# Edge counting of a graph layer: border groups copied by GpSimd, last counts and decode rearranged, hints at a branch

## The chip, the cores and the metric

The program runs on one core of one Trainium2 chip. A core has five engines that run their own instruction streams and meet at semaphores: TensorE (PE in the profile; its weight loads are PEld), VectorE (DVE), ScalarE (ACT), GpSimd (POOL) and SyncE (SP, which here issues most DMAs). The metric is the time of one execution on the device in microseconds. A run's time is the span of the profiled instructions and a little around it.

## The reference, cut to what matters

The network is a two-layer graph attention network on 625 nodes with 20000 edges, followed by a transformer block with a mixture of experts. The change lies in the first part of the first graph layer:

```python
ei = _add_self_loops(edge_index, n)             # 20000 edges, sorted by dst, and 625 loops
src, dst = (ei[0], ei[1])
xl = (x @ W).reshape(n, heads, out_ch)          # x is layer-normalized; 625x768 @ 768x1024
alpha_src = jnp.einsum('nhc,hc->nh', xl, a_src)
alpha_dst = jnp.einsum('nhc,hc->nh', xl, a_dst)
e = jax.nn.leaky_relu(alpha_src[src] + alpha_dst[dst], 0.2)
m = jax.ops.segment_max(e, dst, num_segments=n)
e = jnp.exp(e - m[dst])
s = jax.ops.segment_sum(e, dst, num_segments=n)
msg = xl[src] * (e / (s[dst] + 1e-16))[:, :, None]
out = jax.ops.segment_sum(msg, dst, num_segments=n)
```

The same layer also needs the residual product `h0 @ Wr1 + br1`, of the same size as `x @ W`.

## The kernel before

The kernel has no list of edges in its attention. It first builds a dense matrix `C` of 625 x 625 counts (how often source s points at target d), held as five tiles of 125 targets, and then does attention as dense work with `C` as a weight: a score is masked where `C` is 0 and its exponential is multiplied by `C`.

**Counting.** The edges are laid out as 160 columns of 125 edges, in `G` = 40 groups of `GJ` = 4 columns, sorted by target. For one column, `count` (line 258) makes two small matrices and multiplies them on PE into the accumulator `cps`, five PSUM banks, one for each tile of targets: `target` (line 254, always DVE) makes `oh`, a 125 x 125 one-hot row of the target with a weight, and `step` (line 246) makes a 125 x 210 step function of the source, on ACT or on DVE. The sum over edges of steps, differenced along the columns, is a histogram. To need 210 columns instead of 625, three thirds of the sources share a column with the weights 1, 256 and 65536 (`places`, line 263, gives weight and place), and `decode` (line 492) takes the three fields apart again with rounding on DVE and ACT.

A group goes to the tile in which its first target lies; its index is read into a register of PE (`some`, line 434). A group that reaches over the border between two tiles must be counted for the next tile too. `overlaps` (line 328) finds for each of the four borders the last group that begins below it: it makes a one-hot row `selg` over the groups, GpSimd multiplies it into the three arrays `past`, `upper` and `dst` (twelve products), and DVE reduces these to `rest`. The 16 columns of `rest` are the last counts.

**What runs between the counts.** The first 90 us of the span interleave the counts with the layer norm (`deviation`, `normalized`), the transposes of the normalized rows (`turn_y`), the product with W1 (`project1`: for each of 5 tiles two halves of 512 columns, 12 products in the trace for each half), the sums with the attention vectors (`dots`, DVE) and their transposes (`spread`). PE, DVE and ACT are under a manual schedule here: their instructions stand in the order in which the code calls them, so an instruction that waits holds up all behind it on its engine. `oh` and `step` tiles come from rings of `AHEAD` = 24 buffers. All PSUM results of this stage that aren't counts use three buffers, `pps`.

After the last counts the code runs `residual1(0)`, the decode of the five tiles, `residual1(1)` and the first scores of tile 0 (`lifted`, ACT and then DVE). Each `residual1` is one half of the residual product of tile 0, 12 products in the trace; what it returns is ACT's copy of the result to `pr`, called later.

**The branch.** `examine` tests that the edges are sorted and that no pair occurs so often that a field overflows. If not, the `If` at line 536 counts again in a safe way, 2684 instructions over the engines that this input never runs; every engine reads `oki` and jumps over its own part. Behind it stand `Messages` of tile 0 (`neg` at line 589, the masked maximum at 596, exp at 599, the weighing at 602), `project_residual(1)` on PE (`ph`, line 173) and the transposes of the weighed scores (`tpz`, line 616).

## Time and profile before

| | us |
|---|---|
| median of 3 runs | 1011.8 (1011.01 to 1015.82) |
| the profiled execution | 1011.31 |
| its span | 1009.0 |
| PE busy in the span | 958.5 |
| DVE, ACT, POOL busy | 457.9, 297.3, 68.4 |
| counting stage up to the last count | 0 to 90.9 |
| decode (first copy of `cps` to last field) | 93.7 to 104.6 |
| first transposes of weighed scores, `tpz` | 120.9 |

In the lists in order of time a row gives the start and the duration in us, the engine, the line, the operation with what it writes and reads, its shape, and in brackets how long the engine had been idle and what ended that. Instructions of one form that follow each other are one row (x12), whose duration runs from the first start to the last end. The duration of one DVE or ACT instruction is longer than its distance to the next, since neighbours overlap by some tenths of a microsecond. Fields that end in q (PEq) are an engine's instruction sequencer.

### The profile page before, as it was taken

What the parts mean: (1) busy time and instruction counts of PE and PEld (TensorE: products, weight loads), DVE (VectorE), ACT (ScalarE), POOL (GpSimd) and SP (SyncE); (2) the same over time, 40 slices, a digit from 0 to 9 for tenths busy, and PEclk for the clock granted to TensorE, in tenths of its full rate; (3) what the DMA queues carried; (4) which work ended last, traced back from release to release, by engine and by line L of the source; (5) the groups of instructions that cost most, each with busy time, mean ns of one, the idle gap of its engine ahead of it and who ended that gap; (6) DMA issues with size and microseconds to landing.
All of it is one profiled execution on the core that took longest, in us unless ns stands there. A gap on an engine that the chain in (4) does not pass through costs nothing. (4 is left out here: it accounts for less than half of the span.)

```text
span 1009.0 us, 15158 instructions
## 1 busy us (share of the span) xinstructions
PE 958.5 (95%) x4655; PEld 588.9 (58%) x4656; DVE 457.9 (45%) x1331; ACT 297.3 (29%) x777; POOL 68.4 (7%) x140
## 2 busy tenths in 40 slices
PE   7999799999999999999999889999999999989995
PEld 4565464777655556677775555545455655544553
DVE  8888775584194840485555454121210122221303
ACT  4897552552131120444442211002110212011302
POOL 1000000000000010000000022110100110200001
PEclk9999899999999999999999789999999999999998
DMA  9404100301410174999300579500489999999994
GB/s 276 161 1 168 34 1 24 117 1 46 87 24 1 55 182 83 404 406 379 136 2 1 222 221 358 168 18 25 162 316 317 353 366 408 341 403 365 406 404 156
DMA packets 87726, 191.69 MB, mean 190 GB/s; under 512 B 34404, under 2 KB 36316, under 8 KB 87673
## 3 DMA queue, kind: packets, MB, share of 16 engines
q1 hardware_dynamic: 80441, 175.22, 49.0%
q0 software_dynamic: 7152, 15.64, 5.3%
q8 instruction: 29, 0.48, 0.2%
q10 hardware_dynamic: 80, 0.16, 0.1%
q14 instruction: 24, 0.20, 0.1%
HBM read 213.29 MB, written 39.55 MB: 251 GB/s over the span
## 5 line engine op out<-in xcount | busy, mean ns | idle before, releaser
L1309 PE MATMUL pw<-ew,hT 128*64 128x384 f32 (+1 forms) x672 | 160.1, 487 | 6.3 <-PEq L1629 2.1
L1309 PEld LDWEIGHTS pw<-ew,hT 128*64 128x64 f32 (+1 forms) x672 | 101.3, 160 | 59.5 <-issue 15.3
L1283 PE MATMUL ph<-ew,xid 128*64 128x512 f32 (+1 forms) x432 | 127.7, 594 | 3.4 <-DMA ew<-in_L_ffn_W_dram 1.8
L1299 ACT ACTIVATE hT<-tph,bT 128x64 f32<-128x64 f32 (+1 forms) x168 | 41.0, 361 | 289.0 <-PE tph L1294 194.2
L1283 PEld LDWEIGHTS ph<-ew,xid 128*64 128x64 f32 (+1 forms) x432 | 53.6, 155 | 66.8 <-issue 59.7
L1286 DVE COPY hb<-ph 128x512 f32<-128x512 f32 x30 | 20.6, 688 | 139.1 <-PE ph L1283 139.1
L629 PE MATMUL agg<-xl,zT 125*125 125x256 f32 (+1 forms) x300 | 79.8, 417 | 1.5 <-ACT zT L618 1.4
L629 PEld LDWEIGHTS agg<-xl,zT 125*125 125x125 f32 x300 | 54.5, 188 | 19.8 <-ACT zT L618 2.8
L398 PE MATMUL pp<-w,yT 128*125 128x512 f32 x120 | 55.0, 609 | 0.1
L1346 DVE TENSOR_TENSOR rw<-rw,pw 64x192 f32<-64x192 f32 (+1 forms) x48 | 12.9, 315 | 91.0 <-PE pw L1309 90.7
L734 PE MATMUL ph<-wr,h1T 128*125 128x384 f32 x160 | 52.8, 486 | 0.0
L693 PE MATMUL ph<-w,h1T 128*125 128x384 f32 x160 | 52.4, 486 | 0.0
L249 ACT ACTIVATE step<-halved,past 125x210 f16<-125x210 f16 x138 | 50.9, 459 | 0.0
L173 PE MATMUL ph<-wr,yT 128*125 128x512 f32 x96 | 44.9, 625 | 5.2 <-PEq L536 2.8
L958 DVE CUSTOM_DVE_ANT_0 e<-sc,later 125x625 f32<-125x625 f32 (+4 forms) x60 | 29.9, 543 | 36.2 <-PE sc L942 36.2
L1025 PE MATMUL po<-wpj,aT 128*125 128x384 f32 x120 | 42.8, 505 | 0.4 <-DVE xx L1029 0.4
L962 ACT ACTIVATE e<-e,of 125x625 f32<-125x625 f32 (+4 forms) x60 | 35.7, 596 | 23.3 <-DVE of L958 23.3
L693 PEld LDWEIGHTS ph<-w,h1T 128*125 128x125 f32 x160 | 30.0, 188 | 21.1 <-issue 0.5
L734 PEld LDWEIGHTS ph<-wr,h1T 128*125 128x125 f32 x160 | 29.8, 188 | 20.8
L876 PE MATMUL pv<-L_ffn_Wv,hT 128*125 128x384 f32 x120 | 39.5, 486 | 0.0
L913 PE MATMUL pq<-hT,L_ffn_Wq 128*128 128x313 f32 (+1 forms) x144 | 39.4, 429 | 0.0
L913 PE MATMUL pq<-hT,L_ffn_Wk 128*128 128x313 f32 (+1 forms) x144 | 39.4, 429 | 0.0
(350 smaller groups left out, 1278.1 us busy)
## 6 DMA issues: line engine op xcount, KB each, us to landing
ew<-in_L_ffn_W_dram SPq DMA_DIRECT2D x108, 1536.0 KB
xr<-zt SPq DMA_DIRECT2D x5, 3076.0 KB
xg<-zt SPq DMA_DIRECT2D x5, 3072.0 KB
w<-in_L_gnn_W_dram SPq DMA_DIRECT2D x4, 1536.0 KB
wr<-in_L_gnn_Wr_dram SPq DMA_DIRECT2D x4, 1536.0 KB
xid<-xg POOLq DMA_DIRECT2D x40, 96.0 KB, 9.4
b2b<-in_L_ffn_b_dram SPq DMA_DIRECT2D x9, 384.0 KB
rw<-xr POOLq DMA_DIRECT2D x14, 192.2 KB
```

What stands on the lines that cost most here:

```text
L173: nc.tensor.matmul(pp[:R, :], yT[:, c, cols(t)], part(wr1, KD, c, i, 512), start=(c == 0), stop=(c == KD - 1))
L249: nc.scalar.activation(o, halved[:, :n], AF.Sign, bias=at, scale=-1.0)
L398: nc.tensor.matmul(pp[:R, :], yT[:, c, cols(t)], part(w1, KD, c, i, 512), start=(c == 0), stop=(c == KD - 1))
L629: nc.tensor.matmul(self.agg[:R, c0:c0 + n], zT[:, s, :], xl[:, s, x0:x0 + n], start=(s == 0), stop=(s == T - 1))
L693: nc.tensor.matmul(ph[:R, :384], h1T[:, c, cols(t)], part(w2, KH, c, i, 384), start=(c == 0), stop=(c == KH - 1))
L734: nc.tensor.matmul(ph[:R, :384], h1T[:, k, cols(t)], part(wr2, KH, k, i, 384), start=(k == 0), stop=(k == KH - 1))
L876: nc.tensor.matmul(pp[:R, :384], hT[:, c, cols(t)], w[i][:, c, :], start=(c == 0), stop=(c == KD - 1))
L913: nc.tensor.matmul(pp[:, :b - a], w[:, c, c0:c0 + 128], hT[:, c, a:b], start=(c == 0), stop=(c == KD - 1))
L1025: nc.tensor.matmul(po[t, i][:R, :384], aT[:, c, cols(t)], wpj[i][:, c, :], start=(c == 0), stop=(c == KD - 1))
L1283: mm = nc.tensor.matmul(ph[g * M:(g + 1) * M, :C].rearrange("p (j f) -> p j f", f=128), self.xT[:, k, :], w[:, k, g], start=(k == 0), stop ...
L1299: self.made = nc.scalar.activation(hT[c][:, k, r], tp[:, k, r], AF.Relu, bias=self.bT[:, f:f + 1])
L1309: mm = nc.tensor.matmul(pw[i][g * M:(g + 1) * M, :384], hT[c][:, k, g * M:(g + 1) * M], w[:, self.block(c, g, k), i * 384:(i + 1) * 384], ...
```

## The change

- **Border groups.** The arrays `upper`, `past` and `edges` get one more group in front, set to 0 by GpSimd. `overlaps` counts on DVE, with one comparison and one reduce, the groups that begin below each border; GpSimd reads each count into a register and copies that group's four columns out of the three arrays. The reduces and products of before are gone.
- **Last counts.** In tile 4 both copies of `xl` come right after the products. Then follow `residual1(0)`, `dots(4)`, the last three groups, the copy to `pr`, `spread(4)`, the 16 counts of `rest`, and then `residual1(1)`, whose copy to `pr` is called after the decode. The first scores `zs` are made before the decode. `expert_biases` (two transposes, a copy to `bT_all`) stays right before the decode and so stands behind `residual1(1)`.
- **Decode.** ACT copies 210 columns of a tile to SBUF (`s`), and DVE subtracts there. Three tiles are copied before the first subtraction; their steps are then interleaved across tiles.
- **Branch hints.** Two prefetch hints for the `If` are put in the streams of DVE and ACT, beside the last tile's first field. PE's stream gets none.
- **Zero products.** Twenty products of zeros (`WARM`) are added into `cps` after the self loops' counts.
- **Order at the start.** `tl`, `tli` and `drel` come before the layer norm of tile 0, and `places` is split: two operations before the normalized rows, three after.
- `examine` sums within its comparison.

```diff
@@ zero products, arrays with a group of zeros in front
+            for i in range(WARM):
+                nc.tensor.matmul(cps[:, i % T, :SH + 1], zeros[:, :R], zeros[:, :SH + 1], start=False,
+                                 stop=False, skip_group_check=True)
-            edges = etile([2 * G, GJ], "edges")
...
+            edges = etile([2 * G + 1, GJ], "edges")
...
+            padded = {n: etile([G + 1, GJ], n) for n in ("upper", "past")}
+            upper, past = (padded[n][:, 1:, :] for n in ("upper", "past"))
+            for a in (*padded.values(), edges):
+                nc.gpsimd.memset(a[:, :1, :], 0.0)
+            dev = deviation(0)
+            placing = places(src, upper, past)
+            next(placing)
+            y = normalized(0, *dev)
+            for _ in placing:
+                pass
@@ overlaps
-                for t in range(1, T):
-                    below = op_.tile([R, G], F32, name="below", bufs=2)
-                    nc.vector.tensor_scalar(below, tl, float(t), None, op0=OP.is_lt)
-                    nc.vector.tensor_reduce(cnt[:, t - 1:t], below, AX.X, OP.add)
...
-                nc.vector.tensor_tensor(selg, iog, cnt[:, :, None].to_broadcast([R, T - 1, G]),
-                                        op=OP.is_equal)
...
-                        nc.gpsimd.tensor_mul(m, a.rearrange("p g j -> p j g"),
-                                             selg[:, t, None, :].to_broadcast([R, GJ, G]))
-                        parts.append((rest[i][:, t, :], m))
...
+                below = etile([T - 1, G], "below")
+                nc.vector.tensor_tensor(below, tl[:, None, :].to_broadcast([R, T - 1, G]),
+                                        tile_no[:, :, None].to_broadcast([R, T - 1, G]), op=OP.is_lt)
...
+                nc.vector.tensor_reduce(cnt, below, AX.X, OP.add)
+                cnti = op_.tile([1, T - 1], I32, name="cnti", bufs=1)
+                nc.vector.tensor_copy(cnti, cnt[0:1, :])
...
                 for t in range(1, T):
+                    last = nc.values_load(cnti[0:1, t - 1:t], engines=[mybir.EngineType.Pool],
+                                          min_val=0, max_val=G)
+                    for r, a in zip(rest, (padded["past"], padded["upper"], edges)):
+                        nc.gpsimd.tensor_copy(r[:, t - 1, :],
+                                              a[:, ds(last, 1), :].rearrange("p o j -> p (o j)"))
+                    nc.gpsimd.tensor_scalar_add(rest[2][:, t - 1, :], rest[2][:, t - 1, :],
                                                 -float(t * R))
@@ the end of the counting stage
-            for _ in check:
-                pass
-            expert_biases()
-            nc.scalar.activation(small.tile([R, 1], F32, name="sd"), eps[:R], AF.Exp)
-            dots(T - 1)
             copied = residual1(0)
+            dots(T - 1)
+            some(3)
+            copied()
+            spread(T - 1)
+            for t in range(1, T):
+                for j in range(GJ):
+                    count(cps[:, t, :SH + 1], *(r[:, t - 1, j:j + 1] for r in rest), j < GJ - 1)
+            nc.scalar.activation(small.tile([R, 1], F32, name="sd"), eps[:R], AF.Exp)
+            copied = residual1(1)
+            zs = [lifted(rows, al, 0, h) for h in range(HEADS)]
+            for _ in check:
+                pass
+            expert_biases()
@@ decode
-                nc.scalar.copy(d, cps[:, t, 1:SH + 1])
-                nc.vector.tensor_tensor(d, cps[:, t, :SH], d, op=OP.subtract)
+                s = ah.tile([R, SH + 1], F32, name="s", bufs=T)
+                nc.scalar.copy(s, cps[:, t, :SH + 1])
+                yield
+                nc.vector.tensor_tensor(d, s[:, :SH], s[:, 1:], op=OP.subtract)
...
+                    if t == T - 1 and k == 2:
+                        for ins in (lowered.ins, made.ins):
+                            with tc.issue_after(ins):
+                                tc.mark_branch_hint_location("general", hint="LikelyTaken",
+                                                             engines=[ins.engine])
@@ the five tiles
-            copied()
-            spread(T - 1)
-            copied = residual1(1)
-            zs = [lifted(rows, al, 0, h) for h in range(HEADS)]
+            going = [decode(t) for t in range(T)]
+            for d in going[:3]:
+                next(d)
+            for t in range(T + 2):
+                for i in range(min(t, T - 1), -1, -1):
+                    next(going[i], None)
+                if t + 3 < T:
+                    next(going[t + 3])
             copied()
             ok = nc.values_load(oki[0:1, 0:1], min_val=0, max_val=1)
-            with tc.If(ok == 0):
+            with tc.If(ok == 0, label="general"):
```

## The prediction

> **What bounds the kernel now.** I read the page first, then the list of waits of TensorE (PE), then the order of time of the first 165 us, then windows of 1 us and of 3.41 us around the one slow place.
>
> ```profile
> span 1009.0 us, 15158 instructions
> PE 958.5 (95%) x4655; PEld 588.9 (58%) x4656; DVE 457.9 (45%) x1331; ACT 297.3 (29%) x777; POOL 68.4 (7%) x140
> ```
>
> PE is busy 95% of the span. The instructions behind the `If` stand in the same order on every engine in both programs, so only the first 121 us can change, and whatever PE gains there moves the rest with it.
>
> ```profile
> PE tpy L390 <- DVE y L309: 3.8, 1, 3.8
> PE ph L173 <- PEq L536: 2.8, 1, 2.8
> PE ph L173 <- ACT pr L407: 2.3, 1, 2.3
> ```
>
> These are PE's three longest waits (total, times, longest): for the first normalized tile, for the branch of the `If`, for ACT's copy of half a residual. The order of time (start, us, engine, line) shows what surrounds them:
>
> ```profile
> 10.70 1.51 PE L390 MATMUL tpy<-ident,y 125*128 125x125 f32 x6 [3.83 <-DVE y L309]
> 12.15 6.87 PE L398 MATMUL pp<-w,yT 128*125 128x512 f32 x12
> 25.83 0.80 PE L390 MATMUL tpy<-ident,y 125*128 125x125 f32 x6
> ...
> 80.07 5.33 PE L398 MATMUL pp<-w,yT 128*125 128x512 f32 x12
> 85.24 5.74 PE L260 MATMUL cps<-step,oh 125*125 125x210 f16 x36
> ...
> 97.05 5.32 PE L173 MATMUL ppr<-wr,yT 128*125 128x512 f32 x12
> 104.71 1.12 PE L173 MATMUL ph<-wr,yT 128*125 128x512 f32 x2 [2.35 <-ACT pr L407]
> 108.64 12.39 PE L173 MATMUL ph<-wr,yT 128*125 128x512 f32 x22 [2.81 <-PEq L536]
> ```
>
> Twelve 512-wide products take 5.33 us, but 6.87 at 12.15; 22 of them at 108.64 take 12.39 where 22/12 x 5.33 is 9.8. The windows of 1 us (PE, PEld, DVE, ACT, POOL, then the granted clock) say why the second is slow:
>
> ```profile
> 106.00:107.00 1.00, 0.00 (x0) 0.00 (x0) 0.98 (x2) 1.00 (x2) 0.00 (x0) 1.00 0.09 25
> 108.00:109.00 1.00, 0.36 (x1) 0.39 (x2) 0.99 (x2) 0.57 (x2) 0.00 (x0) 0.50 0.03 8
> 113.00:114.00 1.00, 1.00 (x3) 0.44 (x2) 0.96 (x5) 0.68 (x1) 0.33 (x1) 0.50 0.40 129
> 115.00:116.00 1.00, 1.00 (x4) 0.42 (x3) 0.96 (x4) 0.11 (x2) 0.00 (x0) 1.00 0.88 344
> ```
>
> After a thin stretch of PE the clock is 0.50 for some 6.8 us.
>
> **The change, part by part** (times on the clock of the profile before).
>
> *Zero products and the earlier y.* DVE now does `tl` (0.15 + 0.67), `tli` (0.17) and `drel` (0.30) in its 1.6 us wait for x, and only two of `places` (0.15 apart) while ACT makes `sd` (9.13 to 9.42). The reciprocal starts at 9.47 instead of 9.77, so y ends at 10.34, 0.3 earlier. PE is idle from 6.86 to 10.70 now. Twenty zero products at the spacing of the five at L243 ((1.14 - 0.39)/4 = 0.19 us) fill 3.8 of these 3.84 us. PE is then busy from 4.08 on. Before, it was busy from 10.70 on and its products went from 0.85 to 0.43 us apart at about 15.0, so 4.3 us of work suffice. I take full speed from y on: the transposes cost 0.80 instead of 1.51. With y at 10.34 the first copy of `yT` starts near 10.9 and the products near 11.4 instead of 12.15, and the twelve cost 5.33 instead of 6.87: 0.75 + 1.54 = **2.3 us**. If the zeros end late, at 10.7, 0.3 is lost; if the clock doesn't rise, all but 0.3. The weights cover this: by the windows 2.94 MB had arrived by 12.0, and dst, src, x and half of W1 are 2.2 MB; the other half makes 3.75 MB, which had arrived by 14.0 and is wanted at 17.7. The tile still ends on ACT (11 steps, 4.07 us, then the copies of `yT`).
>
> *Border groups on GpSimd.* Gone from DVE: eight `below`/`cntg` (0.16 us apart on average, 1.3), `selg` (0.33), twelve reduces (0.22 apart, 2.7), four adds (0.36), two reduces of `examine` (0.67 each). New: three DVE operations (about 0.8) and, on GpSimd, three small memsets, four register loads, twelve copies of 125x4, four adds. No row shows a GpSimd operation addressed by a register: 0.16 us (the iota of 125x5) below, 0.62 (the largest product there now) above; I take 0.6, nearest to two-input work of this engine, 12 us for 20 steps. They start at 15.3 and are wanted at 93.8, and behind them in GpSimd's queue wait only `be1` and `br1`, wanted after 112. So 0 on the path. The DVE time saved is worth 0 too: tiles 1 to 3 run at 14.3 us each (44.73, 59.06, 73.74) with PE full. Below nothing it can't go while PE hides it; the first tile's wait is ACT's.
>
> *Last counts and decode.* From 80.07, using the rows above: project1 ends at 85.40, eight counts (0.09 apart) and the transposes of `al` end at 86.5, `residual1(0)` runs to 91.75. Meanwhile ACT copies `xl` (0.59), DVE makes `dots(4)` (eight at 0.35, to 88.9), then twelve `oh` and a step (to 92.0); ACT's eleven steps (0.37 apart) end at 91.2. PE's twelve counts and `spread(4)` end at 93.3. Now a new wait: ACT's copy of `rows` stands before its twelve border steps, so these run from 93.85 to 98.3, and PE gets its 16 counts at that pace, to 98.5 (they ended at 90.8). Queued behind them on PE is `residual1(1)` (5.2, to 103.65) and the transposes for `bT_all` (0.25). ACT's `Exp` load (1.28) and four z (0.735 apart) fit in until 102.7. ACT then waits for `bT_all`, so the first copy of `cps` starts at 104.2 instead of 93.69. The decode took 10.9 us (93.69 to 104.60) with gaps on DVE; with three tiles copied ahead it's paced by DVE's five operations, 1.46 us a tile (`d` and `r` 0.60, the other three 0.87, by their starts from 101.55 to 103.01): 0.3 + 5 x 1.46 + 0.5 = 8.1, to 112.3 with ACT's copy of `pr` at its end. The subtraction from SBUF instead of PSUM shows no row; the like one with all in SBUF (L506, 0.37) stands beside 0.38, so 0.
>
> PE takes its branch at 103.9: 2.8 us as now, no hint stands on its queue. The first half of `project_residual(1)` runs 106.7 to 111.8; the second waits for that copy of `pr` (the instruction order gives it this wait) and runs 112.35 to 117.5. DVE meets its branch at 112.2. Its stall now is 2.77 us (109.0 to 111.76, L589); with the hint I take 0.5 (bounds 0 and 2.8, since no row shows a hinted branch here). z of head 0 is complete 3.2 us after `neg` starts (111.76 to 114.99), so at 115.9, before 117.5. Transposes of z thus start at 117.5 instead of 120.87: **3.4 us**. DVE then lags PE by some 3.4 us more than before; it idles 1.1, 1.5, 1.3 and 1.8 us at 122, 141, 143 and 148, and no part of its work comes later than in the profile before, so I count nothing there.
>
> *Sum*: 2.3 + 3.4 = 5.7. The profiled execution took 1011.31 (span 1009.0 and 2.3 around it), so 1005.6; the median of the runs is 0.5 above it, so **1006.1**.
>
> *The clock* is the open term. PE in the 16 counts does 1.4 us of work in 5.2, with no pause over 0.6. Windows of 3.41 us on the grid of the drop (114.05) give both ends: 103.81 to 107.22 with 1.12 us busy lost the clock, 837.67 to 841.08 with 1.56 busy (46%) kept it, but 557.78 to 561.19, with tiny products, lost it at 2.10. Bounds 0 and 3.4 us (a drop of 6.8). I take 0, as the counts never stop for long, and give the other end a large chance.
>
> The Trainium skill ("TensorE: Matmul & The Clock Gate", Part 1 on the clock gate) says that the clock falls after an idle window of about 3.4 us. By this rule the counts keep the clock and the sum is 5.7. Here the window at 103.81 was a third busy and lost it all the same, so the rule alone doesn't settle it.
>
> **The rivals.**
>
> *The clock falls in the counts.* Then `residual1(1)` runs at half speed for 3.4 to 5.2 us of its time and the decode starts 1.7 to 3.4 late; or it falls at PE's branch, 2.8 idle, and the half of `project_residual(1)` behind it loses 1.7, of which 0.5 is covered. Gain 2.3 to 4.0: 1007.8 to 1009.5. For it speaks the window at 103.81; against it, 837.67.
>
> *The hints do nothing.* DVE stays 2.8 at its branch, z of head 0 comes at 118.2, of head 1 at 119.9; PE waits 0.7 and then some 1.7: gain 3.3, 1008.5. For it: the stalls on PE and DVE are alike (2.81, 2.77) and both begin when the engine has finished its own work, so more than a fetch may be in them.
>
> *GpSimd is late* (slower). If a step with a register costs c, the borders are ready at 15.3 + 20c and wanted at 93.8: it decides from c = 3.9 us on, six times the 0.62 of the row. It is slower by 0.5% from c = 4.5 on; at 5 us it is 21.5 late, 1027.6. Only the lack of any such row speaks for it.
>
> **How the numbers follow.** A measurement of this kernel can tell about 0.5% (5 us) from no change. Forecast 0.55 (own range 1003, where the border steps hold PE up less, to 1007.5, where the zero products bring 0.9; most of it below 1006.7), clock 0.28, no help of the hints 0.10, GpSimd 0.07. Faster: 0.50 from the forecast and 0.03 from the edges of the others, 0.53; same: 0.05 + 0.27 + 0.08 = 0.40; slower 0.07. The range leaves out GpSimd and a little at each end: 1002.0 if the border steps didn't pace PE at all (PE's own work ends 4 us earlier), 1010.7 halfway between the clock's far end alone (1009.5) and with the hints' 2.4 on top (1011.9).
>
> **What would show it.** Right: `tpy` at 10.4 with 0.8 us and its products 5.3; 16 counts spread over 5 us beside ACT's steps; the first copy of `cps` near 102 and `neg` near 110.5 on the new clock, idle before it under 1 us; transposes of z near 115.2; clock 1.00 throughout. Wrong: a 0.50 window between 90 and 116; PE waiting for `rest`; DVE still 2.8 idle at L544; the second half of `project_residual(1)` not waiting for `pr`, which would make it faster than I say.

## The result, and the profile after

The changed kernel takes 1014.7 us (median of 20 runs, 1012.29 to 1018.23), beside 1011.8 for the kernel before (20 runs): a ratio of 1.0029, 95% interval 1.0017 to 1.0040. The forecast was 1006.1 with a range from 1002.0 to 1010.7, so the change is 2.9 us slower where 5.7 faster was forecast. The profiled execution took 1013.89 us, 2.6 more than that of before: 1.3 in the span (1010.3) and 1.3 outside it (3.6, before 2.3).

The page, and from the list of PE's waits the two longest and the one for ACT's steps:

```profile
span 1010.3 us, 15200 instructions
PE 962.9 (95%) x4675; PEld 592.1 (59%) x4676; DVE 451.7 (45%) x1309; ACT 297.3 (29%) x777; POOL 64.3 (6%) x147
```

```profile
PE ph L174 <- ACT pr L410: 3.2, 1, 3.2
PE agg L637 <- ACT zT L626: 2.7, 5, 1.5
...
PE cps L261 <- ACT step L250: 1.6, 2, 1.0
```

The waits for `y` (now 0.4) and for the branch are gone from the top; a wait for `zT`, 0.3 at this place before, has grown to 1.5. PE in order of time (start, us, engine, line):

```profile
10.43 0.86 PE L393 MATMUL tpy<-ident,y 125*128 125x125 f32 x6 [0.39 <-DVE y L316]
11.53 5.42 PE L401 MATMUL pp<-w,yT 128*125 128x512 f32 x12 [0.24 <-ACT yT L387]
...
92.10 4.47 PE L261 MATMUL cps<-step,oh 125*125 125x210 f16 x16 [1.03 <-ACT step L250]
96.36 6.22 PE L174 MATMUL ppr<-wr,yT 128*125 128x512 f32 x12
102.42 0.33 PE L433 MATMUL tb<-ident,bb 96*128 96x96 f32 x2
102.89 5.38 PE L174 MATMUL ph<-wr,yT 128*125 128x512 f32 x12
111.51 7.11 PE L174 MATMUL ph<-wr,yT 128*125 128x512 f32 x12 [3.23 <-ACT pr L410]
118.46 0.71 PE L624 MATMUL tpz<-ident,z 125*125 125x125 f32 x5
119.64 0.81 PE L624 MATMUL tpz<-ident,z 125*125 125x125 f32 x5 [0.48 <-DVE z L610]
121.98 4.11 PE L637 MATMUL agg<-xl,zT 125*125 125x256 f32 x10 [1.53 <-ACT zT L626]
...
133.49 1.88 PE L174 MATMUL ph<-wr,yT 128*125 128x512 f32 x4
```

The start is 2.1 us earlier (`tpy` of tile 1 is at 23.76, before at 25.83), where 2.3 was forecast. The transposes `tpz` start at 118.46, 2.4 earlier than before. By the next residual product all of it is lost: it begins at 133.49, where the kernel before had it at 132.23. From the first `tpz` to the first `agg` it is 3.5 us; before it was 1.5:

```profile
120.87 1.25 PE L616 MATMUL tpz<-ident,z 125*125 125x125 f32 x10
122.41 2.42 PE L629 MATMUL agg<-xl,zT 125*125 125x256 f32 x10 [0.29 <-ACT zT L618]
```

Three rows of twelve or ten products are too long, 6.22, 7.11 and 4.11 us, where the same products take 5.32, 5.38 and 2.32 at full clock. Windows of 1 us (PE, PEld, DVE, ACT, POOL, granted clock, then DMA) show why:

```profile
95.00:96.00 1.00, 0.98 (x4) 0.70 (x4) 0.00 (x0) 1.00 (x3) 0.00 (x0) 0.50 0.00 0
112.00:113.00 1.00, 1.00 (x2) 0.33 (x1) 0.00 (x0) 0.00 (x0) 0.00 (x0) 0.50 0.04 16
123.00:124.00 1.00, 1.00 (x4) 0.81 (x3) 1.00 (x2) 0.93 (x2) 0.00 (x0) 0.50 0.00 0
```

Between 90 and 130 us the clock falls three times, for 3.4 us each, and each time behind a thin stretch of PE; before it fell there once, for 6.8 us. And ACT in order of time shows what `agg` waits for:

```profile
118.90 0.82 ACT L607 ACTIVATE z<-z,m 125x625 f32<-125x625 f32 x1 [0.89 <-DVE m L606]
120.54 0.82 ACT L607 ACTIVATE z<-z,m 125x625 f32<-125x625 f32 x1 [0.82 <-DVE m L606]
121.27 0.66 ACT L626 COPY zT<-tpz 125x625 f32<-125x625 f32 x1
```

The transposes of head 0 are done at 119.17, but their copy stands in ACT's queue behind the fourth exponential, and that waits for DVE's fourth maximum. DVE is late for two reasons: its last work ahead of the branch ends at 111.40 (before at 108.99), and its stall at the branch did not shrink:

```profile
114.72 0.49 DVE L597 TENSOR_SCALAR neg<-C 125x625 f32<-125x625 f32 x1 [3.32 <-DVEq L544]
```

### The profile page after: what moved, and what is told of

The parts are those of the page before. It is cut to its first block, busy times and chain, and to the rows that moved or that the text cites. A ratio compares the mean times of both kernels' runs of the same rounds, so it can differ in the third digit from the quotient of the medians.

```text
span 1010.3 us, 15200 instructions
## 1 busy us (share of the span) xinstructions
PE 962.9 (95%) x4675; PEld 592.1 (59%) x4676; DVE 451.7 (45%) x1309; ACT 297.3 (29%) x777; POOL 64.3 (6%) x147
## 5 line engine op out<-in xcount | busy, mean ns | idle before, releaser
L742 PEld LDWEIGHTS ph<-wr,h1T 128*125 128x125 f32 x160 | 29.8, 188 | 20.8
```

What stands on the lines that cost most here:

```text
L742: nc.tensor.matmul(ph[:R, :384], h1T[:, k, cols(t)], part(wr2, KH, k, i, 384), start=(k == 0), stop=(k == KH - 1))
```

## The experiments

All ran in five rounds beside the kernel before. As the time outside the span turned out to differ between kernels, each result has the median span and the median of what lies outside it. The kernel before has spans of 1008.8 to 1010.5 in these comparisons with 1.9 outside; the changed kernel has 1012.0 and 3.3. Since the span of one and the same kernel moves by 1.7 us between comparisons, a difference of a microsecond between kernels of different comparisons is not shown; where it matters, the span is given against the before of the same comparison. For the changed kernel that is about 2.1 longer (an estimate: the before's 1011.8 less its 1.9 outside is 1009.9).

### The parts alone

**Order at the start and zero products, put alone into the kernel before:**

```
+WARM = 20                       # 20 zero products behind the self loops' counts
-            dev = deviation(0)  # before tl
...
+            dev = deviation(0)  # behind drel; places() split around normalized(0)
```

> The kernel before with only the start of the change: twenty zero products, the tile numbers ahead of the layer norm, places in two parts. In the first runs the time outside the profiled span was 1.9 us for the kernel before and 3.3 to 3.6 for all kernels with the zero products, 1.6 without them. My theory: the zero products take 2.2 us out of the span (1010.5 to 1008.3) and put 1.5 us on the time outside it, so the time is 1011.2 to 1012 against 1012.4 before. Rival: the time outside the span belongs to something else in the change; then it stays at 1.9 and the time is near 1010.2.

Measured: 1011.5 us, ratio 0.9997 (0.9986 to 1.0008); span 1007.4, 1.4 shorter than the before's in this comparison, but 3.7 outside. In its profiled execution the first products of tile 4 start at 73.73, as before (73.74), since the clock falls on the way:

```profile
28.59 7.11 PE L407 MATMUL pp<-w,yT 128*125 128x512 f32 x12
```

The part gains in the span less than its 2.2 us, and all that it gains is lost again outside.

**The changed kernel without its zero products** (`WARM = 0`):

> The changed kernel without the twenty zero products. My theory: the zero products work as predicted, so without them the transposes of the first normalized rows take 1.5 us and the first twelve products 6.9, and the time rises by 1.5 to 2.5 us to 1016.2 to 1017.2. Rival: what starts earlier is lost again at the decode (the clock falls at another place); then the time changes by less than 0.7 us.

Measured: 1016.1 us, ratio 1.0042 (1.0029 to 1.0056); span 1014.35, 1.6 outside. Against the before of its comparison the span is 3.85 longer, and 3.45 in `zero_in_if` below, the other kernel that doesn't run the products; with them it is some 2.1. So the zero products are worth 1.4 to 1.8 us of the span (`start_only` has 1.4), and 1.7 comes back outside. The six spans here lie between 1010.6 and 1016.2, so these sizes are rough.

**The border groups, put alone into the kernel before** (the new `overlaps`, padded arrays, `tile_no`):

> The kernel before with only the border groups copied by GpSimd. My theory: nothing of it is on the path in the first 80 us; at the last counts VectorE has 1.5 us less to do ahead of its last one-hots (five reduces and the adds), so they end 0.5 to 1.5 us earlier, and the time is 0 to 1.5 us less than before. Rival (GpSimd late with its register loads and copies): TensorE waits for rest and the time rises by more than 2 us.

Measured: 1011.0 us, ratio 1.0004 (0.9995 to 1.0013); span 1009.2, 1.6 outside. The 36 last counts run from 85.09 in 5.74 us, as before. Worth nothing, as forecast. In the changed kernel's trace GpSimd's 16 operations, with the register loads between them, lie between 16.34 and 20.78 us, some 0.22 us a step where I took 0.6.

### The branch

**Without the hints:**

```
-                    if t == T - 1 and k == 2:
-                        for ins in (lowered.ins, made.ins):
-                            with tc.issue_after(ins):
-                                tc.mark_branch_hint_location("general", hint="LikelyTaken", ...)
```

> The changed kernel without its two branch hints. My theory: the hints do nothing useful, since VectorE idled 3.3 us at the branch with one and 2.8 without one before the change; without them VectorE's idle time at the If is 2.7 to 3.0 us and the time is 0 to 0.6 us less than the changed kernel's 1014.7, so 1014.1 to 1014.7. Rival: the hint does shorten a stall that would be longer now, so the idle time grows to 4 us or more and the time rises by 1 us or more.

Measured: 1014.7 us, ratio 1.0028 (1.0016 to 1.0040), span 1011.65, 3.5 outside: no different from the changed kernel.

```profile
114.95 0.49 DVE L592 TENSOR_SCALAR neg<-C 125x625 f32<-125x625 f32 x1 [3.49 <-DVEq L539]
```

The stall is 3.49 without and 3.32 with the hint.

**The load of `oki` into registers moved ahead of the decode** (hints kept):

> The changed kernel with the register load of oki on all engines moved from behind the decode to before it, the branch left where it is. If most of VectorE's 3.3 us at the If is the fetch of the code behind it, its idle time stays above 2 us and the time falls by less than 1 us from 1014.7. Rival: the load of the register is a large part of the 3.3 us; then the idle time falls to 1 to 2 us and the time by 1.5 to 2.5 us, since the scores of tile 0 come that much earlier.

Measured: 1012.5 us, ratio 1.0013 (1.0001 to 1.0025); span 1009.0, 3.6 outside.

```profile
114.48 0.49 DVE L597 TENSOR_SCALAR neg<-C 125x625 f32<-125x625 f32 x1 [2.76 <-DVEq L544]
121.74 2.42 PE L637 MATMUL agg<-xl,zT 125*125 125x256 f32 x10 [1.52 <-ACT zT L626]
```

So some 0.6 us of the stall is the register load, and 2.8 us is the branch itself, hint or not. The kernel before has the load in the same place and yet waits 2.77: there DVE's compare for the branch is issued at 108.8, before DVE's last operation ends (108.99), and in the changed kernel at 111.7, behind its end (111.40). The time fell by 2.2 us (by 1.6 against the before of the comparison), the rival's size, though the stall fell only by 0.6. In this execution the clock did not fall at `agg` (2.42 instead of 4.11); whether it holds there in the other runs isn't known. The Trainium skill ("Runtime: NRT & Kernel Launch", Instruction fetch mechanics) says that a taken branch to a place outside the window of fetched instructions makes the engine wait for a fetch; a stall of 2.6 to 2.9 us in every kernel whose load stood earlier agrees with that, and no run here shows a hint that shortens it. PE's own stall of 2.8 us is gone in the changed kernel (at most 0.15), without a hint. Its trace has PE's compare for the branch at 96.6, while the products of `residual1(1)` ahead of it run until 102.58; that this hides the stall is likely, but no experiment isolates it.

### What sets the start of the decode

**`expert_biases` behind the decode**, so that ACT's first copy of `cps` no longer waits for the transposes behind `residual1(1)`:

```
-            expert_biases()      # ahead of the decode
...
             copied()
+            expert_biases()
```

> The changed kernel with the two transposes and the copy of bT_all called after the decode, so that ACT's first copy of cps no longer waits for residual1(1) on TensorE. My theory (the chain from the last count through decode, branch and scores of tile 0 sets the end): the first copy starts 2.3 to 2.7 us earlier, near 100.4, the first agg product near 119.5 instead of 122.0, and the time falls by 2 to 4 us, to 1010.7 to 1012.7. Rival (TensorE's own clock drops and its wait for pr set the end): the first agg comes less than 1 us earlier and the time falls by less than 1 us.

Measured: 1012.4 us, ratio 1.0009 (0.9997 to 1.0021); span 1008.9, 3.1 shorter than the changed kernel's, 3.55 outside.

```profile
109.33 5.42 PE L174 MATMUL ph<-wr,yT 128*125 128x512 f32 x12 [0.92 <-ACT pr L410]
115.86 0.78 PE L624 MATMUL tpz<-ident,z 125*125 125x125 f32 x5 [1.12 <-DVE z L610]
```

The whole chain moves by 2.2 us (`neg` 112.48; the first `agg` at 119.75, as expected), the wait for `pr` shrinks to 0.92, and the clock holds at 109.33. Now `tpz` waits for `z`: DVE's chain is next. Behind it the clock falls all the same (`agg` takes 4.63).

**All steps of the last 16 counts on DVE instead of 12 on ACT:**

> The changed kernel with all sixteen steps of the border groups made by VectorE (twelve were ACT's, behind its copy of rows). My theory (the last counts are paced by ACT's steps behind that copy): the last count ends 1.5 to 2.5 us earlier than 96.6, ACT is free for the Exp table and the four z 4.4 us earlier, the clock does not fall in the counts, and as the copy to bT_all follows residual1(1), the first agg comes 2 to 4 us earlier; time 1011 to 1013. Rival: VectorE, with twelve more steps (2.2 us), becomes the pace and the last count comes no earlier; then the time changes by less than 1 us.

Measured: 1015.4 us, ratio 1.0043 (1.0031 to 1.0055); span 1010.4, 4.3 outside. The last count comes 1.2 us earlier, so ACT's steps did set their pace; now DVE's do, 0.41 us apart. The clock falls all the same, against the expectation (`residual1(1)` takes 6.84), the first copy still waits for `bT_all`, and `neg` starts at 114.39. The span is shorter; the run is slower by what lies outside.

### The clock

**Two zero products behind each of the last 16 counts:**

```
+                    for i in range(2):
+                        nc.tensor.matmul(cps[:, t, :SH + 1], zeros[:, :R], zeros[:, :SH + 1],
+                                         start=False, stop=False, skip_group_check=True)
```

> The changed kernel, with two products of zeros behind each of the 16 last counts, 32 in all: 32 x 0.09 = 2.9 us of work in the 5.2 us that ACT's steps need anyway. Thin windows take the clock (theory): no granted clock of 0.50 between 90 and 111, residual1(1) takes 5.3 instead of 6.22 us, the copy of bT_all and so the first copy of cps come 0.9 earlier (102.1), neg near 113.8, and the span is about 0.9 shorter than the changed kernel's; the time outside the span stays between 3.3 and 4.3, so that the ratio lies near 1.002 to 1.003. Rival, the clock falls there for another reason than PE's idle time: residual1(1) stays at 6.2 us and the span as it was or longer, by what the extra products delay the counts.

Measured: 1012.1 us, ratio 1.0005 (0.9993 to 1.0017); span 1010.5, 1.6 outside.

```profile
98.31 5.33 PE L174 MATMUL ppr<-wr,yT 128*125 128x512 f32 x12
```

```profile
97.00:98.00 1.00, 1.00 (x14) 1.00 (x13) 0.00 (x0) 0.98 (x3) 0.00 (x0) 1.00 0.00 0
```

`residual1(1)` takes 5.33 instead of 6.22 and the granted clock is 1.00 throughout the counts. It had fallen there because PE did little work in that stretch: 16 x 0.09 = 1.4 us in 4.5 by the spacing of the products (the records, which last longer than the spacing, show 2.03 us busy of the 3.41 before the fall). The pauses between the counts are some 0.3 us; the one of 1.03 us ahead of them stands in this run too (93.81), and the clock held. In all nine profiled executions of the changed kernel and its variants that leave these counts in their place, without the fill, the clock fell there. That the clock falls behind thin work is shown. Against the before the span is 1.1 longer, so 1.0 better than the changed kernel's, as expected. The time outside fell as well, which I had not expected.

### The time outside the span

**The zero products moved into the `If`, where they never run:**

> The changed kernel with its twenty zero products moved into the body of the If, which this input never runs: TensorE's stream is as long as in the changed kernel, but none of them is executed. If the time outside the span depends on where TensorE's code lies (the length of its stream), it is 3.3 to 3.6 us as in the changed kernel, with a span like that without zero products (1014.3), so 1017.5 to 1018. If it depends on the products being executed, it is 1.6 us and the time 1016.

Measured: 1016.5 us, ratio 1.0063 (1.0041 to 1.0084); span 1012.25, 3.6 outside. The products don't run and the time outside stays. The span is 2 us shorter than expected, but so is the before's in this comparison (1008.8): it is 3.45 longer than that, close to `no_zero`'s 3.85.

**The kernel before with 20 never-run products in its `If`** (nothing that runs is changed):

> The kernel before, with twenty products of zeros written into the body of the If, which this input never runs; nothing that runs is changed, and PE's stream of instructions is 40 longer. Place of code (theory): the span stays at the before's (1008.8 to 1010.5 in the runs so far) and the time outside the span grows from 1.9 to 3.3 to 3.7 us, so the ratio is about 1.0016. Rival, the time outside the span comes from something in the border groups, the decode or the order at the start: the time outside stays at 1.9 and the ratio is 1.000.

Measured: 1012.7 us, ratio 1.0014 (1.0000 to 1.0028); span 1008.9, 3.5 outside. The kernel before gets the changed kernel's time outside from code alone.

**The changed kernel with a safe count shorter by 40 instructions:**

```
                 for a in range(0, EJ, PART):
-                    clear(SH2 + 1)
+                    if a >= 4 * PART:
+                        clear(SH2 + 1)
...
-                                             start=False, ...
+                                             start=q == a and a < 4 * PART, ...
```

> The changed kernel with nothing that runs altered; only the never-run safe count in the If is 40 instructions of PE shorter (its first four parts start their sums in their first product instead of behind five products of zeros). Place of code (theory): the span stays near the changed kernel's 1012.0, the time outside the span falls from 3.3 to 1.6 to 1.9, the ratio from 1.0029 to about 1.0012 to 1.0020. Rival, the time outside the span belongs to something that the changed kernel runs: 3.3 outside as before, ratio 1.003.

Measured: 1014.2 us, ratio 1.0034 (1.0019 to 1.0050); span 1012.55, 1.9 outside. The time outside falls as expected, but the ratio does not: the spans of this run spread from 1008.7 to 1016.6, and their median is 0.55 longer than the changed kernel's. The profiled one lost 1.6 us at 28 us, as `start_only` did.

**The kernel before with 32 never-run products:**

> The kernel before with 32 never-run products of zeros in the If: PE's stream is 64 instructions longer, nothing that runs differs. If any lengthening beyond some point costs: 3.5 us outside the span or more, ratio 1.0015. If it hangs on where the code lies against blocks of 64 instructions (4529, 4530, 4469 and 4601 instructions gave 1.6 to 1.9 and have the remainders 49, 50, 53 and 57; 4569 and 4570 gave 3.3 to 4.3 and have 25 and 26): the remainder is 50 again, 1.9 outside, ratio 1.000.

Measured: 1012.0 us, ratio 1.0006 (0.9993 to 1.0018); span 1010.1, 1.9 outside. Longer code costs nothing here. The expectation has one number wrong: the stream of `fill_counts` is 103 instructions longer than the before's, not 71, so its remainder by 64 is 25 and blocks of 64 were refuted by it already. Sorted by the length of PE's stream against the before's, all kernels of this study give:

| PE's stream against before | kernels | us outside the span (medians) |
|---|---|---|
| 61 shorter | best_b | 1.6 |
| within 1 | before, no_zero, border_only, after_trim, best_a, best_zt, best_pr, best_fill | 1.6 to 1.9 |
| 39 or 40 longer | changed kernel, start_only, no_hints, ok_early, bias_late, steps_dve, zero_in_if, pad_only, zt_early | 3.3 to 4.3 |
| 64 longer | pad_64 | 1.9 |
| 103 longer | fill_counts | 1.6 |

That code that never runs moves the time outside by 1.5 us, both ways, is shown by `pad_only` and `after_trim`. It is not the length as such. Nor is it fixed by the code alone: single runs jump between the two values, and five of the changed kernel's twenty have 1.5 to 1.9. What rule picks 40, and on which side of the span the time lies, stays open.

### Behind the branch

**ACT's copy of `zT` of head 0 ahead of the fourth exponential:**

```
+            def last_head():
+                h = HEADS - 1
+                msgs[0].mass(h - 1, zs[h - 1])
+                msgs[0].turn(0)
+                msgs[0].peak(h, zs[h])
+                msgs[0].mass(h, zs[h])
...
-            project_residual(1)
+            project_residual(1, last_head)   # its additions on DVE come behind last_head
```

> The changed kernel with ACT's copy of the first transposed scores (zT of head 0) before the exponential of head 3 instead of behind it; DVE's three additions of the bias to the residual follow the maxima of that head. Copy behind the exponentials (theory): zT is copied when its transposes end, at 119.2 instead of 121.27, agg starts near 120.0 instead of 121.98, PE has no thin stretch there and the clock stays 1.00, so its first ten products take 2.4 instead of 4.1: 2.0 + 1.7 = 3.7 us of the span, 1008.3, with 3.3 outside: 1011.6, ratio about 0.9995. Rival, what waits is DVE's chain (the maximum of head 3, the new neg, the biases), and it is late by the same time a few products on: less than 1 us gained, ratio 1.002 to 1.003.

Measured: 1011.7 us, ratio 1.0012 (0.9997 to 1.0027); span 1007.7, 4.3 shorter than the changed kernel's, 3.8 outside.

```profile
120.78 0.71 PE L624 MATMUL tpz<-ident,z 125*125 125x125 f32 x5
121.95 0.81 PE L624 MATMUL tpz<-ident,z 125*125 125x125 f32 x5 [0.46 <-DVE z L610]
122.64 2.42 PE L637 MATMUL agg<-xl,zT 125*125 125x256 f32 x10
```

From the first `tpz` to the first `agg` it is 1.9 us instead of 3.5, `agg` waits for nothing, and the clock holds (2.42 instead of 4.11). This confirms the place of the loss behind the branch. Against the before of the comparison the span is 1.6 shorter, so 3.7 better than the changed kernel's, as expected. In the trace 2.7 of it shows up to the next residual product (12.3 us from the first `tpz`, instead of 15.0); where the rest comes from isn't located. (This execution, too, lost 1.6 us at 28 us.)

### Put together

**best_a**: the changed kernel without hints, with the early register load, `expert_biases` behind the decode, the 16 last counts ahead of the copies of `pr` and `rows`, and the safe count trimmed.

```
+            for t in range(1, T):        # ahead of copied() and spread(T - 1)
+                for j in range(GJ):
+                    count(cps[:, t, :SH + 1], *(r[:, t - 1, j:j + 1] for r in rest), j < GJ - 1)
             copied()
             spread(T - 1)
```

> The changed kernel without hints, with the register load before the decode, expert_biases behind the decode, the 16 last counts before the copies of pr and rows, and with a shorter safe count in the If: the first four parts start their sums in their first product instead of behind five products of zeros, so that PE's stream is one instruction shorter than the before's. The decode's start sets the end (theory): ACT's border steps start near 90.2 instead of 91.6, the last count ends near 95.1, the first copy of cps starts near 100 instead of 103.0, neg near 111.2 instead of 114.72, the span is some 4.4 shorter than the changed kernel's, near 1007.6. Place of code: 1.6 to 1.9 outside the span, so a time near 1009.3 and a ratio near 0.998. Rivals: the clock falls elsewhere and takes 1 to 2 us of it (ratio 0.999 to 1.000); or the time outside the span follows what the start runs, and is 3.5 again (ratio 1.000).

Measured: 1006.9 us, ratio 0.9961 (0.9948 to 0.9975); span 1005.2, 1.7 outside. `neg` starts at 110.63 [2.65], 4.1 earlier than in the changed kernel, and the clock no longer falls in the counts. The span is some 2 us shorter than expected. `agg` again waits for `zT`:

```profile
108.10 6.96 PE L174 MATMUL ph<-wr,yT 128*125 128x512 f32 x12 [3.04 <-ACT pr L410]
114.89 1.48 PE L621 MATMUL tpz<-ident,z 125*125 125x125 f32 x10
117.90 2.42 PE L634 MATMUL agg<-xl,zT 125*125 125x256 f32 x10 [1.53 <-ACT zT L623]
```

**best_b**: the same with the safe count shorter by 100 instead of 40.

> As best_a, with all ten parts of the safe count without their products of zeros: PE's stream is 61 instructions shorter than the before's, and nothing that runs differs from best_a. If the time outside the span grows with the length of PE's stream: 1.9 or less outside, ratio 0.998 as best_a. If it depends on where the code happens to lie (a boundary in the instruction memory), it can be 3.5 here though the stream is shorter: ratio 1.000.

Measured: 1007.5 us, ratio 0.9963 (0.9950 to 0.9975); span 1005.5, 1.6 outside. The same time, but the two traces differ at 28 us, where both run the same instructions. The row of best_a:

```profile
28.23 5.41 PE L401 MATMUL pp<-w,yT 128*125 128x512 f32 x12
```

and that of best_b:

```profile
28.57 7.07 PE L401 MATMUL pp<-w,yT 128*125 128x512 f32 x12
```

The traces settle why. The clock changes only at whole steps of 3.41 us, counted from its first change in the execution, and these steps lie differently against the program each time: in best_a the clock rises at 8.83 us, in best_b at 11.45. So the thin stretch ahead of the products is shared by two steps in best_a and falls into one step in best_b. The first row is the emptier of best_a's two steps there, with PE busy for 2.50 us; the second is the step before best_b's fall, with 2.08:

```profile
25.90:29.31 3.41, 2.50 (x11) 1.59 (x12) 3.41 (x18) 3.41 (x11) 0.00 (x0) 1.00 1.01 386
25.10:28.52 3.42, 2.08 (x11) 1.15 (x10) 3.42 (x18) 3.42 (x11) 0.00 (x0) 1.00 1.03 404
```

**best_zt**: best_a with the earlier copy of `zT`.

> best_a with the same earlier copy of zT. Theory: agg starts near 116.4 instead of 117.9, so 1.5 us of the span go (the clock was 1.00 there already): span 1003.7, 1.7 outside, ratio 0.9946. Rival, DVE's chain is late next: nothing gained, ratio 0.996.

Measured: 1005.6 us, ratio 0.9948 (0.9930 to 0.9967); span 1003.85, 1.9 outside.

```profile
116.39 1.53 PE L621 MATMUL tpz<-ident,z 125*125 125x125 f32 x10
117.93 2.42 PE L634 MATMUL agg<-xl,zT 125*125 125x256 f32 x10
```

From the first `tpz` to `agg` it is 1.5 us instead of 3.0, as in the theory.

**best_pr**: best_zt with the copy of `pr` in the middle of the decode, which takes away the wait that the prediction's gain was counted from.

```
                 if t + 3 < T:
                     next(going[t + 3])
+                if t == 3:
+                    copied()
-            copied()
```

> best_zt with the copy of residual1(1) to pr in the middle of the decode instead of at its end. PE's wait for pr sets the end (as the prediction counted it): the second half of project_residual(1) starts near 107.4 instead of 109.44 and ends near 112.8 instead of 116.4, and up to 3 us of the span go: 1000.8, ratio 0.992. DVE's chain sets the end (theory): z of head 0 is complete at 115.4 all the same, so PE waits 2.6 us before tpz instead of 3.0 before ph, the clock falls there and the transposes and the first agg run at half speed: agg starts near 117.6 and ends later than best_zt's 120.2; span 1003.5 to 1005.5, ratio 0.995 to 0.996.

Measured: 1006.35 us, ratio 0.9939 (0.9921 to 0.9956); span 1004.65, 1.7 outside.

```profile
107.54 5.42 PE L174 MATMUL ph<-wr,yT 128*125 128x512 f32 x12 [0.55 <-ACT pr L410]
115.89 0.78 PE L622 MATMUL tpz<-ident,z 125*125 125x125 f32 x5 [2.94 <-DVE z L608]
```

The wait moves from 3.0 us before `ph` to 2.9 before `tpz`. The span is no shorter (against the before of the comparison 5.75 less, in best_zt 5.45; the intervals overlap). PE's wait for `pr` was cover for DVE's chain, not the bound.

**best_fill**: best_zt with two zero products behind each of ten counts at 24 to 28 us, and a safe count shorter by as many instructions.

```
-                    some(3)
+                    some(3, 0 if t else 10)   # fill: two zero products behind a count
```

> best_zt with two products of zeros behind each of the first ten of the 12 counts at 24.4 to 28.2 us, and a safe count shorter by as much, so that PE's stream has best_zt's length. In the profiled executions of six of the twelve kernels with the zero products at the start the clock fell to 0.50 from about 28 to 32 us, and project1's twelve products took 7.1 instead of 5.4. Thin windows take the clock (theory): 1.8 of PE's 3.8 us there are filled, the fall is gone in every execution, the span is 0.9 shorter in the mean (half of the executions by 1.8) and less spread: about 1003.0 and a ratio of 0.994. Rival, the fall there has another cause (the transfers of weights at 400 GB/s, a phase of the clock's windows that products don't change): products at 28 take 7.1 in some executions as before, span 1003.8, ratio 0.995.

Measured: 1004.0 us, ratio 0.9921 (0.9901 to 0.9942); span 1002.25 (mean 1002.3, of best_zt 1003.8), 1.85 outside; its six spans lie between 1000.6 and 1004.0, those of best_zt between 1000.0 and 1006.2.

```profile
27.86 5.42 PE L401 MATMUL pp<-w,yT 128*125 128x512 f32 x12
...
107.71 5.41 PE L174 MATMUL ph<-wr,yT 128*125 128x512 f32 x12 [3.04 <-ACT pr L410]
113.86 0.78 PE L625 MATMUL tpz<-ident,z 125*125 125x125 f32 x5 [0.73 <-DVE z L611]
```

This is the fastest kernel of the study by its median, 0.8% faster than before, but its interval overlaps best_zt's, so the worth of the fill itself isn't settled. The clock was 1.00 in every window of 1 us from 20 to 130 us of its profiled execution. At 28 us the fill does it: the two steps of the clock there have PE busy for 3.07 and 3.40 of 3.41 us. At the wait for `pr` it is luck: a step ends at 105.77, in the middle of the wait, and leaves 2.31 and 1.48 us busy in the two steps, where best_a has 0.64 in one (104.41 to 107.82) and lost the clock. So it need not hold in other runs.

## Why the prediction was wrong, step by step

*The start* (2.3 us): right in its mechanism and, in the profiled execution, in its size: `tpy` at 10.43 with 0.86 us, products at 11.53 in 5.42, tile 1's products 2.07 earlier. The twenty products took 3.2 us, not 3.8, and left 0.4 idle, which did no harm. What I left out is that the same thin counts at 24 to 28 us that cost nothing before can now take the clock. It fell there in seven of the thirteen profiled executions that ran the zero products without the fill, and in none of the six without them; each fall takes 1.4 to 1.8 us of the gain (from the normalized rows of tile 1 to the first products of tile 4 it is 49.2 to 49.6 us with it and 47.8 without). Which of the two happens goes with where the steps of the clock lie: it rose at 8.83 to 9.60 us in the six that kept it and at 10.59 to 11.86 in the seven that lost it. In `start_only` 1.4 of the 2.3 is left in the medians.

*Border groups* (0): right. The rival that GpSimd is late falls: the borders are ready at 20.8 us and wanted from 88.1 on, by DVE.

*Last counts and decode*: right but for the clock. ACT's copy of `rows` held up its border steps, the last count ended at 96.57 (forecast 96.2 on the new clock), and ACT waited for `bT_all`. `residual1(1)` took 0.9 longer at half speed, so the first copy of `cps` came at 103.0 (101.9) and the decode took 8.4 us (8.1): the copy of `pr` ended at 111.45 instead of 110.0.

*The clock as an open term*: taken as 0, with 0 and 3.4 us as its bounds. This is the first step that failed, and its bound was too small, because I looked for one fall and there were three: 0.9 in `residual1(1)`, 1.8 in the second half of `project_residual(1)`, 1.7 in `agg`. The rival named the first place; its other one, behind PE's branch, kept the clock, and the fall came one half later, behind the wait for `pr`. My reason for 0, that the counts never stop for long, is refuted by `steps_dve`, where the last ones stop for some 0.3 us at a time and the clock falls, and by `fill_counts`, where more work keeps it: what counts is how full a stretch is, not how long its pauses are.

*The second half waits for `pr`*: it does (3.23 us). But it was the wrong quantity to count from. Transposes of `z` came 2.4 us earlier than before instead of 5.7; 1.5 of the difference is the later copy and 1.8 the clock.

*PE's branch, 2.8 us as before*: failed, at most 0.15, but without effect on the sum, since the second half waits for `pr` either way.

*DVE's branch, 0.5 us with the hint*: failed, 3.32, beyond my upper bound of 2.8, with 0.6 for the register load in it. The rival that the hints do nothing is right on its mechanism (`no_hints`). It was priced at 2.4 us because I followed it only to the first `tpz`.

*What no part of the prediction had*: "no part of its work comes later than in the profile before, so I count nothing there". `neg` came at 114.72, 3 us later than before, and the copy of `zT` stands behind four exponentials. That added 2.0 us to `agg` (`zt_early`).

The account of the profiled execution closes: 5.7 forecast, less 3.3 at `tpz` (118.46 against 115.2), less 2.0 before `agg`, less 1.7 in `agg`, is -1.3 us, and the span is 1.3 longer.

*The time outside the span, taken as unchanged at 2.3*: failed, 1.3 us in the profiled execution and 1.4 in the medians. The prediction never asked what forty more instructions do to a program beside their running time.

## What to carry to other kernels

Follow a late engine through its queue to the next thing that somebody else needs, not to the first wait that it causes: a wait of PE that looks like the bound can be the cover of a chain on another engine, and taking it away only moves it. Look at each thin stretch of PE in the stage, those that the change makes and those that it merely shifts, and price a fall of the clock at each; cheap work that fills them is worth trying. One profile doesn't tell whether such a stretch costs: it can keep the clock in one execution and lose it in the next. And when spans and times disagree, test padding alone.

## What the runs showed of the hardware

- A trickle of products takes the clock without any long pause. In `steps_dve` the last counts stand 0.41 us apart with pauses of some 0.3 us, and the clock falls at 94.79. With two more products in each pause it stays (`fill_counts`).
- In every trace here the clock changes only at whole steps of 3.41 us: in the changed kernel it rises at 9.39 and falls at 94.72, 111.79 and 122.03, which are 25, 30 and 33 steps later. Read on these steps, the seven executions that lost the clock at 28 us lost it behind a step with PE busy for 1.9 to 2.1 us by the records, and the six that kept it have 2.5 us or more in both steps there. Busy time alone is not the rule: `no_zero` lost the clock behind a step with 2.48 (94.20 to 97.62), and best_fill kept it behind one with 1.48.
- The Trainium skill ("TensorE: Matmul & The Clock Gate", Part 1) says that the window of some 3.4 us in which activity is watched runs freely and doesn't start with the kernel, so that the moment of a change differs from run to run. These traces agree. The same section puts a fall behind an idle window, which is too narrow for these runs, where steps more than half busy took the clock too.
- The same wait of 3.0 us for `pr` cost the clock in best_a and best_zt (6.96 and 7.11 us) and not in best_fill (5.41), where a step of the clock ended within the wait.
- A taken branch costs DVE 2.6 to 3.0 us. With the register load right before it, it is 3.3 to 3.6 in the kernels with the changed order and 2.8 to 3.0 in those with the order before. A hint in the stream some 3 us ahead changed nothing (3.32 with, 3.49 without).
- Forty never-run instructions moved the median time outside the span from 1.9 to 3.5 us; 64 did not, nor did a stream longer by 103.
- GpSimd's copies of 125x4 addressed by a register start 0.12 to 0.13 us apart, and a register load between them costs some 0.5 us.
